# The outlook stage of a two-layer metaformer kernel: norm, outer and band moved in the step's order, loads moved to ScalarE's queue, the last stage's factors loaded and folded in two pieces

## The chip, the cores and the metric

One core of one Trainium2 chip runs the whole kernel. The metric is device time in microseconds for one execution, as a median of runs. The engines are named as the profile names them: PE (TensorE; PEld its weight loads), DVE (VectorE), ACT (ScalarE), POOL (GpSimd) and SP (SyncE, which here only issues DMAs). ACT and POOL can issue DMAs too; those stand in the engine's own stream of instructions, between its other work. The profile calls the DMA queue of SP q1, that of ACT q10 and that of POOL q0.

## The reference

The input is four images of 32 x 32 tokens with 384 channels, f32. Layer 0 adds a gated attention and a mixture of four experts; the change does not touch them. Layer 1 adds an outlook attention and a feed-forward network whose weights are Kronecker products. Cut to these two:

```python
x = x + _L1_conv_ref(_ln_c(x), L1_conv_Wv, L1_conv_Wa, L1_conv_Wo)
t = t + _L1_ffn_ref(_ln_t(t), c_fc_1, c_fc_2, c_proj_1, c_proj_2)

def _L1_conv_ref(x, Wv, Wa, Wo):          # 12 heads of 32, K = 3
    v = x @ Wv.T                          # padded by 1 on each side
    v_unf = patches(v)                    # the 3 x 3 neighbours of each pixel
    a = (x @ Wa.T).reshape(b, n, 12, 9, 9)
    attn = softmax(a * 32 ** -0.5)        # over the last 9
    out = einsum('bnhpq,bnqhd->bnphd', attn, v_unf)
    y = fold(out)                         # each of the 9 results is added at its pixel
    return y @ Wo.T

def _L1_ffn_ref(x, fc_1, fc_2, proj_1, proj_2):
    h = gelu(x @ kron(fc_1, fc_2).T)      # fc_1 1536 x 32, fc_2 1 x 12
    return h @ kron(proj_1, proj_2).T     # proj_1 32 x 1536, proj_2 12 x 1
```

## The kernel before

The 4096 tokens are 32 tiles of 128 (P), eight to an image (NB = 8, NT = 32). Four stages follow one another: `attention`, `experts`, `outlook` and `Kron.run`. Within outlook the order of instructions on every engine is the order in which the program emits them (`manual_schedule`, L2346); each engine works through its own list in order, and so do the queues of DMAs.

**What a tile goes through.** `norm` (L1866) writes xn, the layer norm of the tile, on DVE (L147). `turn` transposes it on PE (L155) and copies it to xnT on ACT (L156). `scores` multiplies xnT by wa in two halves of 486 columns (L1881) into the PSUM tiles ps_a0 and ps_a1, one buffer each, and subtracts the maximum of nine on DVE (L1887, L1888). `exps` is one exponential on ACT over the whole tile (L1895). `values` makes v (L1928, copied by ACT in L1932). `share` divides by the sums on DVE (L1901 to L1908) and sends thirds of the result, shifted by one image row (32 partitions), to tiles `up` and `down` with up to four DMAs on SP's queue (L1918, L1919, L1920, L1922): L1918 fills the last 32 rows of the tile before. `outer` copies two pieces of down and up into u on ACT (L1942, L1943), `inner` adds the three others on DVE (L1949 to L1951). `band` shifts u by one column on PE (L1960), masks it on DVE into co (L1968), writes co to a `room` in DRAM (L1975, 150 KB), waits for that on SP, and reads the room back as a band of 260 columns for each token (L1981, 1560 KB). `sort` copies the band, heads in pairs, into `own` with three ACT copies (L1991). `gather` multiplies v by own (L2004) and gathers into ps_y for a half image; with the last tile of a half it copies ps_y into y on ACT (L2013). `mix` multiplies y by wo (L2019), and `mixed` adds it to x (L2026).

**The loop** (L2039 to L2093) runs steps 0 to 36. Step i works on scores, exps, turn(i+1), values and share of tile i, on outer, inner and band of tile i-2, and on sort and gather of tile i-4 (LAG = 4). Mixes come in steps 9 to 15, 17 to 23, 25 to 31 and 33 to 36. Steps 8, 16, 24 and 32 have a gather for t = 4, the last tile of a first half, and two more at the step's end for the second half (L2075). From step 4 on, `add` adds the experts' results to the tiles 17 to 31 on DVE (L1844); POOL fetches them ahead (`ask`, L1541).

**Loads.** `loads` (L2339) is called at the start of a step: at step 1 x for image 1 and wo, at step 2 x for image 2 (from two sources), at step 5 x for image 3, at step 8 `kron.load` (L2117), which loads the factors of the last stage and folds two of them on DVE: f2sum (L2127), row (L2130) and wide (L2132). All of these DMAs stand on SP's queue, between those of share and band. The x tiles of image 0, wa and wv come on POOL's queue ahead of the loop.

**Semaphores of the DMAs.** DMAs on the queues of SP and ACT raise one of eight semaphores. A DMA which takes a semaphore again first waits on the engine that issues it, until the earlier DMA on that semaphore has landed.

The order before, cut to what the change moves:

```python
if 0 <= i - LAG < NT: sort(i - LAG)
if 0 <= i - 2 < NT: outer(i - 2)
if i < NT: scores(i, 0); scores(i, 1); exps(i)
if 0 <= i - 2 < NT: inner(i - 2)
if i + 1 < NT: xn = norm(i + 1)
...                                   # mixes, gather, turn(i + 1, xn), values, share
if 0 <= i - 2 < NT: band(i - 2)
```

Of the kernel before, what the change touches and what calls it, by code (L numbers as in the profile page):

```python
# [17 lines left out]
P = 128  # L18
# [3 lines left out]
NT = B * NB  # L22
# [1744 lines left out]
def outlook(net, wv, wa, wo, left, router, kron, loads):  # L1767
# [10 lines left out]
    tc, nc = net.tc, net.nc  # L1778
# [4 lines left out]
    with ExitStack() as ctx:  # L1783
# [82 lines left out]
        def norm(i):  # L1866
            xn = work.tile([P, C], FP, name="xn", tag="xn")
            net.ln_apply(xn, i, i, net.mv, net.rs)
            return xn
# [69 lines left out]
        def outer(i):  # L1939
            u = us[i] = work.tile([P, 6, 5, H3], FP, name="u", tag="u")  # L1940
            down, up = halves(i)
            nc.scalar.copy(u[:, :, 0, :], down[:, :, 0, :])  # L1942
            nc.scalar.copy(u[:, :, 4, :], up[:, :, 2, :])  # L1943
# [95 lines left out]
        for step in range(last + 1):  # L2039
            i = step  # L2040
            if step in loads:
                loads[step]()
            if 0 <= i - LAG < NT:
                sort(i - LAG)
            if 0 <= i - 2 < NT:
                outer(i - 2)
            if i < NT:
                scores(i, 0)
                scores(i, 1)
                exps(i)  # L2050
            if 0 <= i - 2 < NT:
                inner(i - 2)
            if i + 1 < NT:
                xn = norm(i + 1)
            done = []
            for one in mixes.pop(step, []):
                done.append(mix(*one))
                if len(done) == 2:
                    mixed(*done[0])
                    mixed(*done[1])  # L2060
                    gauged += [j for j, _ in done]
                    done = []
            if 0 <= i - LAG < NT:
                gather(i - LAG, 0 if (i - LAG) % NB < 5 else 1)
            if i + 1 < NT:
                turn(i + 1, xn)
            for one in done:
                mixed(*one)
                gauged.append(one[0])
            if i < NT:  # L2070
                values(i)
                share(i)
            if 0 <= i - 2 < NT:
                band(i - 2)
            if 0 <= i - LAG < NT and (i - LAG) % NB == 4:  # L2075
                gather(i - LAG - 1, 1)
                gather(i - LAG, 1)
            if coming:
                add()
                if left and left[0] % NB == 0 or not left and not coming:  # L2080
                    until = left[0] if left else NT
                    net.scale(first, until)
                    first = until
            if step >= 3 and left:
                ask(left.pop(0))
            while gauged and gauged[0] < kron.GT:
                kron.gauge(0, gauged.pop(0))
            if step == 2 * NB + LAG + 3:
                kron.begin(0)
            elif step > 2 * NB + LAG + 3 and t_kron < kron.GT:  # L2090
                for _ in range(2):
                    kron.shrink(0, t_kron)
                    t_kron += 1  # L2093
# [3 lines left out]
class Kron:  # L2097
# [8 lines left out]
    A, K = 32, 12  # L2106
# [10 lines left out]
    def load(self, fc1T, fc2, proj1T, proj2):  # L2117
        nc, A, K = self.nc, self.A, self.K
        const = self.const
        p2 = self.p2  # L2120
        for q in range(4):
            nc.sync.dma_start(out=self.wf[A * q : A * q + A, :], in_=fc1T)
        nc.sync.dma_start(out=self.wp, in_=proj1T.rearrange("(f p) a -> p f a", p=P))
        nc.sync.dma_start(out=self.f2, in_=fc2.rearrange("a b -> (a b)").partition_broadcast(P))
        nc.sync.dma_start(out=p2, in_=proj2.rearrange("a b -> (a b)").partition_broadcast(P))
        self.f2sum = const.tile([P, 1], FP, name="f2sum")
        nc.vector.tensor_reduce(self.f2sum, self.f2, AX.X, ALU.add)  # L2127

        row = const.tile([P, A], FP, name="row")
        nc.vector.tensor_reduce(row, self.net.ident.rearrange("p (q a) -> p a q", a=A), AX.X, ALU.add)  # L2130
        self.wide = const.tile([P, A, K], FP, name="wide")
        nc.vector.tensor_tensor(  # L2132
            self.wide, row.unsqueeze(2).to_broadcast([P, A, K]), p2.unsqueeze(1).to_broadcast([P, A, K]),
            ALU.mult,
        )
        self.xr = [const.tile([P, self.GT, A], FP, name=f"xr_{g}", tag=f"xr_{g}") for g in range(NT // self.GT)]
# [155 lines left out]
@with_exitstack  # L2292
def metaformer_kernel(
    ctx: ExitStack,
    tc: tile.TileContext,
    x, qkv_wT, gpT, proj_wT, proj_w, gate_w, gate_b, wup, wdown,
    WvT, WaT, WoT, fc1T, fc2, proj1T, proj2, out,
):
    cpool = ctx.enter_context(tc.tile_pool(name="cpool", bufs=1))
    small = ctx.enter_context(tc.tile_pool(name="small", bufs=2))  # L2300
    dram = ctx.enter_context(tc.tile_pool(name="dram", bufs=1, space=bass.MemoryType.DRAM))
    net = Net(tc, cpool, small)
    net.slots(dram)
    x1, x2 = (dram.tile([NT * P, C], FP, name=n) for n in ("x1", "x2"))
    unsafe = cpool.tile([1, 1], mybir.dt.int32, name="unsafe")

    def routing(outer):

        pool = outer.enter_context(tc.tile_pool(name="rt", bufs=1))
        ps_t = outer.enter_context(tc.tile_pool(name="ps_t", bufs=2, space=PSUM))  # L2310
        return Router(net, pool, cpool, lambda: ps_t.tile([P, 512], FP, name="ps_t", tag="pt"))

    def rest(router, done):

        with ExitStack() as late:

            pool = late.enter_context(tc.tile_pool(name="late", bufs=1, reuse_waits="tile"))
            kron = Kron(net, late, pool)
            net.xs = {}
            net.home(pool, 0)  # L2320
            wa, wv, wo = (
                pool.tile([P, KC, w.shape[-1]], FP, name=n, tag=n)
                for n, w in (("wa", WaT), ("wv", WvT), ("wo", WoT))
            )
            for b in range(1, B):
                net.home(pool, b)

            def fetch(b):
                first, last = b * NB, (b + 1) * NB
                net.load(x2, range(first, min(last, done)))  # L2330
                net.load(x1, range(max(first, done), last))

            def weigh(queue, tile_, w):
                queue.dma_start(out=tile_, in_=w.rearrange("(k p) o -> p k o", p=P))

            net.load(x2, range(NB), tc.nc.gpsimd)
            weigh(tc.nc.gpsimd, wa, WaT)
            weigh(tc.nc.gpsimd, wv, WvT)
            loads = {  # L2339
                1: lambda: (fetch(1), weigh(tc.nc.sync, wo, WoT)),  # L2340
                2: lambda: fetch(2),
                5: lambda: fetch(3),
                8: lambda: kron.load(fc1T, fc2, proj1T, proj2),
            }
            eng = mybir.EngineType
            with tc.manual_schedule(engines={eng.PE, eng.DVE, eng.Activation, eng.SP, eng.Pool}):  # L2346
                outlook(net, wv, wa, wo, range(done, NT), router, kron, loads)
            kron.run(out)

    with ExitStack() as outer:  # L2350
        router = routing(outer)
        eng = mybir.EngineType
        with tc.manual_schedule(engines={eng.PE, eng.DVE, eng.Activation, eng.SP}):
            left = attention(
                net, outer, router, x, x1, unsafe, qkv_wT, gpT, proj_wT, proj_w, gate_w, gate_b
            )
            done = experts(net, router, x1, x2, wup, wdown, left)
    rest(router, done)
    with tc.If(tc.nc.values_load(unsafe[0:1, 0:1], min_val=0, max_val=1) != 0):
        with ExitStack() as outer:  # L2360
            net.reside(outer.enter_context(tc.tile_pool(name="xpool", bufs=1)))
            net.load(x)
            general_attention(net, qkv_wT, gpT, proj_wT)
            net.store(x1)
            with ExitStack() as inner:
                router = routing(inner)
                for b, given in enumerate(gates(net, router.psum, gate_w, gate_b)):
                    for _ in router.route(b, *given):
                        pass
                    if b == B - 2:  # L2370
                        router.first()
                done = experts(net, router, x1, x2, wup, wdown, router.schedule)
        rest(router, done)
# [59 lines left out]
```

## Time and profile before

| | us |
|---|---|
| median of three runs (2775.6 to 2779.86) | 2779.47 |
| the profiled execution's own time | 2777.38 |
| its span, first to last instruction | 2774.9 |
| attention, to about | 1204 |
| experts, to about | 2250 |
| outlook, first turn to the start of step 9 | 2250.31 to 2371.64 |
| outlook, steps 9 to 31, to the last scores | 2371.64 to 2640.0 |
| outlook, steps 32 to 36 | 2640.0 to 2684.24 |
| Kron.run | 2684.24 to 2774.9 |

The mean granted clock of PE is 0.959. In these four last stretches PE is busy for 88.59 of 121.33, 264.17 of 268.36, 36.05 of 44.24 and 78.41 of 90.66 us, and the DMA engines for 60%, 57%, 48% and 20%.

How to read it. A timeline row gives the start, the time of the instruction or of a merged run of them, engine, line, operation and tiles; in brackets stands the time for which the engine had been idle, and what ended that. A row of the windows gives, for a stretch, its length, then busy time and number of instructions of PE, PEld, DVE, ACT and POOL, the granted clock, the share of the DMA engines' time and GB/s. "SPq" and "ACTq" rows are the issuing of DMAs: their time is that of the issue, not of the transfer. Ends of matmuls are modelled, so that the time from one run's start to the next one's is the safer figure.

### The profile page before, as it was taken

To read this page: it belongs to the slowest core of one execution; us is meant where nothing else is said; L and a number is where in the kernel's file an instruction comes from. 1 tells how busy PE (TensorE), PEld (TensorE's weight loads), DVE (VectorE), ACT (ScalarE), POOL (GpSimd) and SP (SyncE) were. 2 spreads that over 40 slices of the span, in tenths; PEclk is the share of its full clock that TensorE was granted. 3 is DMA by queue.
4 is the path that set the end of the run, shared out by engine and by line. 5 is a ranking of instruction groups with operands and counts; after the bars stand their busy time and mean duration, and the time that the engine had idled before them with its cause. 6 is when DMAs were issued, how large, how long until landed. Compare 5 with 4: busy or idle time off the path is not lost. (4 is left out here: it accounts for less than half of the span.)

```text
span 2774.9 us, 40133 instructions
## 1 busy us (share of the span) xinstructions
PE 2565.5 (92%) x14667; PEld 1558.3 (56%) x14667; DVE 1728.3 (62%) x4362; ACT 1301.9 (47%) x2119; POOL 417.8 (15%) x501
## 2 busy tenths in 40 slices
PE   6889999999999998789999999999999987999988
PEld 3323333333333332247889999999999953555532
DVE  1367778677778787647444544465455556887962
ACT  3778777677778777412221221121121123455455
POOL 1000000030003001413211112222222101110000
PEclk9989999999999998889999999999999999999989
DMA  5133434322322232454665545655655447565532
GB/s 108 33 103 92 108 86 126 95 60 63 96 73 64 59 107 69 133 175 160 230 238 207 202 170 216 232 194 217 237 205 211 175 145 221 165 201 175 173 110 93
DMA packets 215806, 404.13 MB, mean 146 GB/s; under 512 B 83344, under 2 KB 176848, under 8 KB 202544
## 3 DMA queue, kind: packets, MB, share of 16 engines
q1 hardware_dynamic: 184496, 187.82, 22.6%
q0 software_dynamic: 26960, 209.05, 22.0%
q10 hardware_dynamic: 4144, 4.61, 0.5%
q8 instruction: 118, 1.93, 0.3%
q14 instruction: 88, 0.72, 0.1%
HBM read 304.34 MB, written 49.00 MB: 127 GB/s over the span
## 5 line engine op out<-in xcount | busy, mean ns | idle before, releaser
L1702 ACT ACTIVATE h<-ps_h,up 128x256 f32<-128x256 f32 (+1 forms) x420 | 195.1, 465 | 825.3 <-PE ps_h L1697 823.7
L1697 PE MATMUL ps_h<-xbT,up 128*128 128x256 f32 (+1 forms) x2520 | 531.1, 371 | 2.5 <-ACT h L1702 1.8
L689 DVE CUSTOM_DVE_ANT_0 e<-e,rz,inv 128x1024 f32<-128x1024 f32 x384 | 475.3, 1274 | 47.3 <-DMA rz<-r_row 47.3
L1697 PEld LDWEIGHTS ps_h<-xbT,up 128*128 128x128 f32 x2520 | 462.6, 191 | 64.6 <-ACT h L1702 2.6
L637 ACT ACTIVATE e<-ps_s,ten 128x1024 f32<-128x1024 f32 x384 | 408.0, 1109 | 66.6 <-PE ps_s L627 40.1
L627 PE MATMUL ps_s<-q,k 32*128 32x512 f32 x1536 | 297.4, 671 | 51.5 <-ACT e L637 35.0
L645 PE MATMUL ps_o<-e,wv 128*32 128x512 f32 x1536 | 227.2, 666 | 40.3 <-DVE wv L696 38.8
L716 POOL DMA_DIRECT2D q<-po x96 | 76.2, 886 | 947.6 <-DMA q<-po 452.9
L645 PE MATMUL ps_z<-e,rt_ones 128*32 128x512 f32 x1536 | 217.1, 639 | 0.0
L373 ACT ACTIVATE below<-tk_left,tk_bound 128x1024 bf16<-128x1024 f32 (+1 forms) x160 | 184.4, 1152 | 52.4 <-DVE tk_bound L379 41.4
L1741 PE MATMUL ps_y<-wsum,hsum 128*128 128x192 f32 x1116 | 196.0, 329 | 9.5 <-DVE hsum L1657 5.2
L627 PEld LDWEIGHTS ps_s<-q,k 32*128 32x128 f32 x1536 | 92.8, 191 | 189.1 <-ACT e L637 92.0
L1741 PEld LDWEIGHTS ps_y<-wsum,hsum 128*128 128x128 f32 x1116 | 182.5, 191 | 13.2 <-DVE hsum L1657 6.6
L1881 PE MATMUL ps_a<-wa,xnT 128*128 128x486 f32 x384 | 162.1, 571 | 0.6 <-ACT xnT L156 0.6
L1745 DVE TENSOR_TENSOR y<-ps_y,y 128x192 f32<-128x192 f32 x155 | 55.5, 358 | 165.5 <-PE ps_y L1741 162.4
L645 PEld LDWEIGHTS ps_o<-e,wv 128*32 128x32 f32 x1536 | 31.5, 112 | 201.0 <-issue 66.1
L288 PE MATMUL ps_t<-xnT,wqkv 128*128 128x512 f32 x288 | 134.6, 607 | 2.4 <-ACT xnT L470 1.7
L1541 POOL DMA_INDIRECT yt<-yg,index x64 | 78.1, 1220 | 375.5 <-DVE x L1844 181.4
L645 PEld LDWEIGHTS ps_z<-e,rt_ones 128*32 128x32 f32 x1536 | 52.2, 117 | 132.0 <-issue 128.8
L1741 PE MATMUL ps_y<-down,h 128*128 128x192 f32 x744 | 126.0, 326 | 0.0
L1741 PEld LDWEIGHTS ps_y<-down,h 128*128 128x128 f32 x744 | 122.6, 190 | 1.6
L1991 ACT COPY own<-band 128x1040 f32<-128x1040 f32 x96 | 101.7, 1125 | 33.2 <-DMA band<-room 30.8
(398 smaller groups left out, 3576.7 us busy)
## 6 DMA issues: line engine op xcount, KB each, us to landing
band<-room SPq DMA_DIRECT2D x32, 1560.0 KB
rz<-r_row SPq DMA_DIRECT2D x48, 512.0 KB
yg<-y SPq DMA_DIRECT2D x67, 192.0 KB
q<-q SPq DMA_DIRECT2D x192, 64.0 KB
k<-k SPq DMA_DIRECT2D x192, 64.0 KB
room<-none SPq DMA_DIRECT2D x64, 192.0 KB
x<-x SPq DMA_DIRECT2D x35, 192.0 KB
o<-in_x_dram SPq DMA_DIRECT2D x33, 192.0 KB
```

Source lines behind the costliest of these rows:

```text
L288: nc.tensor.matmul(ps, lhsT=lhsT(k), rhs=rhs(k), start=k == 0, stop=k == KC - 1)
L373: nc.scalar.activation(junk[:n], left[:n], AF.Sign, bias=bound[:n], accum_out=over[:n])
L627: nc.tensor.matmul(ps[:, half * 512 : half * 512 + 512], lhsT=self.k4[r, u * P : (u + 1) * P], rhs=self.q4[r, :], start=True, stop=True,)
L637: nc.scalar.activation(e, ps, AF.Exp, bias=shift, scale=QK_SCALE)
L645: nc.tensor.matmul(ps[r : r + 32, :], lhsT=lhsT(odd), rhs=self.es[2 * u + odd][:, half * 512 : half * 512 + 512], start=u == 0, stop=u == ...
L689: nc.vector.tensor_tensor_reduce(self.es[m], self.es[m], self.rz, 1.0, self.im["inv"][:, m, self.h : self.h + 1], ALU.mult, ALU.add, self. ...
L1541: self.nc.gpsimd.indirect_dma_start(out=y, out_offset=None, in_=self.net.yg[: first_row(self.complete(i // NB)), :], in_offset=bass.Indire ...
L1697: nc.tensor.matmul(ps, lhsT=up[:, o : o + P], rhs=xbT[:, k, :size], start=k == 0, stop=k == KC - 1,)
L1702: nc.scalar.activation(hs[f // 3][:, f % 3, :size], ps, AF.Gelu, bias=up[:, KC * HID + f : KC * HID + f + 1])
L1741: nc.tensor.matmul(ps, lhsT=left[f], rhs=right[:, f, :], start=f == 0, stop=f == HF - 1)
L1881: nc.tensor.matmul(pa[:, :HW_], lhsT=xnTs[i][:, k, :], rhs=wa[:, k, hh * HW_ : (hh + 1) * HW_], start=k == 0, stop=k == KC - 1,)
L1991: nc.scalar.copy(own[:, pairs], m.rearrange("p t (n h) -> p n t h", h=2)[:, pairs])
```

## The change

Six edits, all in outlook and in what it loads. In the loop `outer(i - 2)` comes ahead of `sort(i - 4)`; `norm(i + 1)` comes ahead of the scores; in the steps past the last tile (32 and 33) `band` comes ahead of `gather`. The loads at steps 1, 2, 5 and 8 are issued by ACT on its own queue. `kron.load` is cut in two: the DMAs stay at step 8, the three DVE operations become `fold` and move to step 14.

```diff
--- before.py
+++ after.py
@@ -2040,18 +2040,18 @@
             i = step
             if step in loads:
                 loads[step]()
+            if 0 <= i - 2 < NT:
+                outer(i - 2)
             if 0 <= i - LAG < NT:
                 sort(i - LAG)
-            if 0 <= i - 2 < NT:
-                outer(i - 2)
+            if i + 1 < NT:
+                xn = norm(i + 1)
             if i < NT:
                 scores(i, 0)
                 scores(i, 1)
                 exps(i)
             if 0 <= i - 2 < NT:
                 inner(i - 2)
-            if i + 1 < NT:
-                xn = norm(i + 1)
             done = []
             for one in mixes.pop(step, []):
                 done.append(mix(*one))
@@ -2060,6 +2060,8 @@
                     mixed(*done[1])
                     gauged += [j for j, _ in done]
                     done = []
+            if i >= NT and i - 2 < NT:
+                band(i - 2)
             if 0 <= i - LAG < NT:
                 gather(i - LAG, 0 if (i - LAG) % NB < 5 else 1)
             if i + 1 < NT:
@@ -2070,7 +2072,7 @@
             if i < NT:
                 values(i)
                 share(i)
-            if 0 <= i - 2 < NT:
+            if 0 <= i - 2 and i < NT:
                 band(i - 2)
             if 0 <= i - LAG < NT and (i - LAG) % NB == 4:
                 gather(i - LAG - 1, 1)
@@ -2119,10 +2121,14 @@
         const = self.const
         p2 = self.p2
         for q in range(4):
-            nc.sync.dma_start(out=self.wf[A * q : A * q + A, :], in_=fc1T)
-        nc.sync.dma_start(out=self.wp, in_=proj1T.rearrange("(f p) a -> p f a", p=P))
-        nc.sync.dma_start(out=self.f2, in_=fc2.rearrange("a b -> (a b)").partition_broadcast(P))
-        nc.sync.dma_start(out=p2, in_=proj2.rearrange("a b -> (a b)").partition_broadcast(P))
+            nc.scalar.dma_start(out=self.wf[A * q : A * q + A, :], in_=fc1T)
+        nc.scalar.dma_start(out=self.wp, in_=proj1T.rearrange("(f p) a -> p f a", p=P))
+        nc.scalar.dma_start(out=self.f2, in_=fc2.rearrange("a b -> (a b)").partition_broadcast(P))
+        nc.scalar.dma_start(out=p2, in_=proj2.rearrange("a b -> (a b)").partition_broadcast(P))
+
+    def fold(self):
+        nc, A, K = self.nc, self.A, self.K
+        const, p2 = self.const, self.p2
         self.f2sum = const.tile([P, 1], FP, name="f2sum")
         nc.vector.tensor_reduce(self.f2sum, self.f2, AX.X, ALU.add)
 
@@ -2327,8 +2333,8 @@
 
             def fetch(b):
                 first, last = b * NB, (b + 1) * NB
-                net.load(x2, range(first, min(last, done)))
-                net.load(x1, range(max(first, done), last))
+                net.load(x2, range(first, min(last, done)), tc.nc.scalar)
+                net.load(x1, range(max(first, done), last), tc.nc.scalar)
 
             def weigh(queue, tile_, w):
                 queue.dma_start(out=tile_, in_=w.rearrange("(k p) o -> p k o", p=P))
@@ -2337,10 +2343,11 @@
             weigh(tc.nc.gpsimd, wa, WaT)
             weigh(tc.nc.gpsimd, wv, WvT)
             loads = {
-                1: lambda: (fetch(1), weigh(tc.nc.sync, wo, WoT)),
+                1: lambda: (fetch(1), weigh(tc.nc.scalar, wo, WoT)),
                 2: lambda: fetch(2),
                 5: lambda: fetch(3),
                 8: lambda: kron.load(fc1T, fc2, proj1T, proj2),
+                14: kron.fold,
             }
             eng = mybir.EngineType
             with tc.manual_schedule(engines={eng.PE, eng.DVE, eng.Activation, eng.SP, eng.Pool}):
```

In the changed kernel's lists, ACT issues the seven loads of step 8 (four of wf, wp, f2, p2) after the copy of v(7) and ahead of outer(6), sort(4) and exps(8). SP's list is the old one without the loads. PE's list differs only in steps 32 and 33. On the eight semaphores, the fourth wf load takes that of the first one, wp and f2 take those of the L1918 and L1919 copies of step 7, and p2 that of the second wf load.

## The prediction

> **What bounds the kernel now.** I read three views, in this order: the slices of the page, a table of windows with one row for each step of the outlook stage (from the start of its scores matmuls to the next), and the timelines of the engines where a row is longer than its work. From the page, two rows of 40 slices of 69.4 us:
>
> ```profile
> PE   6889999999999998789999999999999987999988
> PEclk9989999999999998889999999999999999999989
> ```
>
> PE is busy nearly everywhere; of the stretches that the change touches, slice 33 (2289 to 2359 us) is the weakest, with 7 tenths. The windows: columns are the stretch, its length, busy time of PE, PEld, DVE, ACT, POOL, granted clock, DMA share, GB/s.
>
> ```profile
> 2251.45:2260.84 9.39, 7.45 (x22) 3.72 (x23) 4.66 (x10) 2.74 (x3) 2.43 (x3) 1.00 0.33 93
> 2260.84:2270.12 9.28, 7.35 (x23) 3.62 (x22) 6.66 (x14) 1.97 (x3) 0.00 (x0) 1.00 0.61 197
> 2270.12:2282.46 12.34, 9.75 (x29) 5.43 (x27) 9.49 (x20) 3.10 (x7) 0.00 (x0) 0.86 0.66 209
> 2282.46:2295.00 12.54, 9.95 (x29) 5.48 (x28) 7.91 (x18) 2.81 (x5) 0.00 (x0) 0.86 0.51 169
> 2295.00:2305.85 10.85, 9.43 (x53) 5.19 (x52) 7.38 (x17) 5.08 (x9) 0.00 (x0) 1.00 0.55 186
> 2305.85:2316.71 10.86, 9.79 (x54) 5.20 (x53) 9.60 (x23) 5.18 (x8) 2.52 (x3) 1.00 0.68 215
> 2316.71:2328.42 11.71, 9.78 (x54) 5.20 (x52) 9.33 (x23) 5.51 (x8) 2.15 (x2) 1.00 0.82 251
> 2328.42:2343.71 15.29, 11.54 (x54) 5.99 (x52) 10.55 (x25) 5.64 (x9) 2.51 (x3) 0.89 0.72 245
> 2343.71:2371.64 27.93, 13.04 (x102) 7.46 (x100) 12.00 (x29) 7.47 (x12) 2.25 (x3) 0.69 0.51 134
> ...
> 2383.57:2454.35 70.78, 70.78 (x349) 39.10 (x348) 64.77 (x154) 36.76 (x54) 13.61 (x14) 1.00 0.66 211
> 2454.35:2466.82 12.47, 10.37 (x101) 5.82 (x99) 11.67 (x29) 7.27 (x12) 2.16 (x2) 1.00 0.65 207
> 2466.82:2549.55 82.73, 82.73 (x410) 45.70 (x407) 66.91 (x158) 42.15 (x63) 3.10 (x4) 1.00 0.55 180
> 2549.55:2563.72 14.17, 12.07 (x101) 6.86 (x99) 10.57 (x27) 10.26 (x15) 0.00 (x0) 0.88 0.51 166
> ```
>
> The first nine rows are steps 0 to 8. Steps 10 to 31, the last four rows and what follows to 2640, are PE without a gap (70.78 of 70.78), except steps 16 and 24. So the change can earn only in steps 0 to 8, 16, 24 and at the end. The longest hole, step 8, in the timelines of DVE, PE and SP's queue:
>
> ```profile
> 2359.39 0.17 DVE L2127 TENSOR_REDUCE f2sum<-f 128x1 f32<-128x12 f32 x1 [12.96 <-DMA f<-in_fc_dram]
> ```
> ```profile
> 2364.15 0.87 PE L155 MATMUL ps_tr<-ident,xn 128*128 128x128 f32 x3 [14.89 <-DVE xn L147]
> ```
> ```profile
> 2350.01 3.59 SPq L2124 DMA_DIRECT2D f<-in_fc_dram  x1
> ```
>
> DVE stands 12.96 us at f2sum until a load of 6 KB lands, which was issued behind the band DMA (1560 KB) and the wf and wp loads; max, subtraction and norm of the step queue behind it, and PE stands 14.89 us.
>
> **Warm PE work of a step**, from rows of the chain: scores 4.90, turn 0.35, values 1.94, band 0.91, gather 1.2 to 1.5 (t=4: 0.5 and 1.5), mix 1.94. Floors: steps 0 and 1 7.2 each, 2 and 3 8.1, 4 to 7 9.3, 9.65, 9.65, 9.3, steps 8, 16, 24 10.1.
>
> **Norm ahead of the scores, steps 0 to 3.** xn is then there when PE has finished the scores, so the waits 1.93, 1.93, 2.59, 2.59 of L155 go. What is late next is xnT: behind the scores' end come max and subtraction (1.36), exps 1.01 and the copy 0.48 on ACT, 2.95 in all with hand-overs. PE has turn and values, 2.3, in steps 0 and 1, with band 3.2 in steps 2 and 3. So step 0 takes 8.15 (9.39 before), step 1 8.15 (9.28), steps 2 and 3 8.2 (12.34, 12.54; there also turn and values at the slow clock go, 0.87+3.07 against 0.35+1.94). Gain 1.24+1.13+4.14+4.34 = 10.9. Bounds: 2.4, if steps 2 and 3 get nothing because their up copies land late, to 13 (43.55 less the floors 30.6). DVE's 0.47 for norm now precedes the max; in steps 10 to 31 the max waits for PE (37.3 us in 40 waits), which hides it; uncovered it would cost 0.47 a step.
>
> **Clock.** PE ran slow after idles of 2.59 (values: six in 3.28) and not after 1.93 (2.10); I charge 1.5 us for each new hole above 2.5. The Trainium skill, "TensorE: Matmul & The Clock Gate", Part 1, says that the clock falls after an idle window of about 3.4 us, free-running; by that the hole I expect in step 4 would cost 0 and the sum be 1.5 better, but the rows with 2.59 speak against it.
>
> **Loads on ACT's queue, outer ahead of sort, steps 4 to 7.** The earlier steps now run into the band DMA. A band takes 6.2 to 6.9 from issue to landing (2666.38 to 2672.58; 2311.61 to 2318.5) and SP's queue lands in order: the up copy issued at 2328.54 landed at 2335.23, 0.15 after the band issued at 2326.42. With steps of 8.2, share(2) ends at 2278.8, room(0) is issued at 2280.6, band(0) at 2283.0, it lands at 2289.4, and the first up copy of step 3, issued at 2286.2, lands behind it at 2289.6. In step 4 ACT does outer (0.47), then sort (3.17), then exps; before, sort came first. So own(0) is ready only at 2293.3, with the scores done at 2288.9: PE waits 4 to 5, and step 4 takes 13.8 plus 1.5 of slow clock. From there each step hangs on the ring exps 1.0, share 2.9 to its first third, up copy 2 to 3.5, outer 0.5, sort 3.2: 9.6 to 11.1. I take 10.75, 11.3, 9.7 for steps 5, 6, 7 (fetch(3) beside step 5). Sum 47.0 against 48.7: gain 1.7. Bounds: every step as step 4, 55.2, a loss of 6.5; the floors, 37.9, a gain of 10.8. The loads' own issue costs ACT 0.4 to 0.6 each, beside its waits for DVE.
>
> **Step 8.** DVE's wait goes. ACT now issues seven DMAs ahead of outer(6), sort(4) and exps(8). The trace shows them on SP: 1.86+0.43+3.59+0.45 = 6.3. Beyond that, in the built kernel the fourth wf load waits on the semaphore of the first, wp and f on those of the up copies of step 7. On my clock: v(7) done at 2329.1, wf landed 2333, wp 2334.6, f 2338.6, p 2339; outer and sort to 2342.7 (gather's first third at 2340.6, scores done at 2334.4); exps and three y copies (1.54) and xnT to 2345.2; values, band and the late gathers with 1.5 to 3 of slow clock to 2349: 19.5 against 27.93, gain 8.4. Bounds: ACT standing as long as DVE did, gain 0; no hole, 17.8. I choose between them by the issue rows.
>
> **Steps 16 and 24.** Waits of 2.10 on xn go (in 24 also values at 3.33). ACT's chain then ends at xnT, 2463.2+0.5, beside PE's work; PE's 10.1 plus 0.7 makes 10.8: gain 1.6 and 3.4, together 5 (0 to 6.4).
>
> **Steady steps, outer ahead of sort.** The up copy lands 1.94 after issue at least (2271.53 to 2273.47); its reader, ACT L1943, started unhindered 3.29 after (2634.75 to 2638.04), 4.29 and 5.06 in others, which bounds it above. Taking the step whose scores start at 2431.36: issue at -0.70, outer 0.47, sort 3.17; the gather starts at +6.91 behind mix and wants its last third 1.0 later, so landings up to 4.97 cost nothing. Price 0, bound 2 us over the stage. **fold** at step 14 adds 0.17+0.35+0.56 = 1.1 on DVE, which is free 6.0 of 70.78 in those steps: 0, uncovered 1.1.
>
> **Last two bands.** Band(30) waits for inner(30), whose place on DVE behind the shrink rows (to 2650.6) is unchanged. Band(31)'s room write is issued up to 1 us earlier, but queues behind band(30) (2658.73 to 2665.38), and the last band is issued at 2666.38 today: gain 0.4 (-2.7, by which sort(28) is later, to 0.9).
>
> **Sum.** 10.9+1.7+8.4+5+0.4 = 26.4. The profiled execution took 2777.38 (span 2774.9 and 2.5 around it), 2.1 less than the median 2779.47: 2777.4-26.4+2.1 = 2753. Differences under 0.2% (5.6 us) count as the same.
>
> **Rivals.** (1) Forecast, 2746 to 2760: 0.54. (2) ACT's stall replaces DVE's: step 8 gains 0 to 3; 2758 to 2762: 0.16. For: the semaphores above; against: only the loads' issue, not f's landing, holds ACT. (3) The bands do not collide: steps 4 to 7 near their floors and step 8 at 14: 11+9+14+5 = 39, 2741: 0.13. For: the loads leave SP's queue; against: 6.4 of band, 2.4 of room and the share copies fill about 10 us of each step. (4) The other queue frees nothing: fetch(2) and fetch(3) delay the up copies as on one queue (7.71 with fetch(3), against 1.94), about 3 us in each of four steps: 12 lost, 2765: 0.09. So says the Trainium skill, "DMA: Bandwidth & Descriptors", section "Issuing engines are not separate DMA queues": only issue time is saved. Its section "Queues, rings and completion order" has the engines alternate between queues by packet, by which a small copy passes a large load; no row here shows either. (5) Slower: outer waits for every up copy in all 22 steps 10 to 31 as long as the two late ones (7.71, 6.69; mean 7.2): sort ends at -0.70+7.2+3.7 = +10.2 against +7.9, 2.3 late, 50 lost: 2803. It decides from 27/22 = 1.2 a step, a landing of 6.2. Against: the bounds 3.29 to 5.06. 0.04. (6) No difference, 2779, gains of (1) eaten by the worst of steps 4 to 8: 0.04.
>
> Faster 0.92, same 0.04, slower 0.04. The range 2740 to 2767 leaves out (5), (6) and about a tenth at the lower edge of (3) and beyond.
>
> **What would show it.** Right: no wait of f2sum, no L155 wait on xn in steps 0 to 3, 16, 24; a PE hole in step 4 ended by own L1991; in step 8 a PE hole of 5 to 8 us ended by own, with ACT's DMA issues ahead; steps 10 to 31 gapless at 11.7. Wrong: PE holes in steps 10 to 31 behind own, an ACT hole over 10 us in step 8, or steps 4 to 7 under 10 us.

## The result, and the profile after

| | before | after |
|---|---|---|
| median of 6 runs each, us | 2779.08 (2775.6 to 2785.98) | 2753.47 (2744.2 to 2759.54) |
| the profiled execution | 2777.38 | 2747.41 |
| its span | 2774.9 | 2745.4 |

The ratio of the medians is 0.9905, with a 95% interval of 0.9891 to 0.9919. The forecast was 2753.0, and the profiled execution is 29.97 us shorter: 1.03 before the outlook stage, 25.63 in it (from the first scores to the first matmul of the last stage: 432.79 to 407.16), 2.85 in the last stage, and 0.47 around the span. Only the 25.63 lie where the change acts; the last stage has the same instructions and ran at a granted clock of 0.94 against 0.89 before.

The slices of the page after, PE and granted clock:

```profile
PE   6889999999999998679999999999999998999988
PEclk9989999999989998779999999999999999999999
```

Slice 33 (2265 to 2334 us now) has 8 tenths where 7 stood, its neighbours 9 each; what is left of the holes is in the table by step. Windows after, steps 0 to 8, then 9, 16 and 24; columns as before.

```profile
2250.42:2258.45 8.03, 7.42 (x22) 3.61 (x22) 3.05 (x5) 2.69 (x4) 2.44 (x3) 1.00 0.37 109
2258.45:2266.47 8.02, 7.42 (x21) 3.61 (x22) 6.62 (x14) 1.76 (x4) 0.00 (x0) 1.00 0.91 289
2266.47:2274.97 8.50, 8.45 (x28) 4.53 (x28) 7.37 (x17) 2.23 (x6) 0.00 (x0) 1.00 0.77 241
2274.97:2283.58 8.61, 8.41 (x28) 4.63 (x28) 7.91 (x20) 2.54 (x7) 0.00 (x0) 1.00 0.22 56
2283.58:2299.34 15.76, 11.27 (x53) 5.77 (x52) 10.70 (x25) 5.46 (x10) 0.00 (x0) 0.89 0.68 235
2299.34:2309.08 9.74, 9.74 (x53) 5.21 (x52) 8.07 (x19) 5.63 (x9) 2.52 (x3) 1.00 0.84 252
2309.08:2324.01 14.93, 11.47 (x54) 5.41 (x52) 10.93 (x26) 5.41 (x8) 2.15 (x2) 0.89 0.84 275
2324.01:2333.42 9.41, 9.41 (x53) 5.22 (x52) 7.90 (x20) 5.22 (x7) 2.51 (x3) 1.00 0.61 166
2333.42:2351.91 18.49, 12.53 (x101) 6.91 (x99) 12.81 (x30) 7.93 (x14) 2.25 (x3) 0.82 0.86 250
2351.91:2363.69 11.78, 11.78 (x62) 6.45 (x58) 8.79 (x20) 4.53 (x7) 2.05 (x2) 1.00 0.55 184
...
2434.61:2444.96 10.35, 10.35 (x102) 5.89 (x100) 9.37 (x23) 6.95 (x12) 2.16 (x2) 1.00 0.71 238
2527.65:2538.00 10.35, 10.35 (x101) 5.87 (x99) 7.88 (x21) 9.93 (x17) 0.00 (x0) 1.00 0.60 199
```

PE's first busy figure is the step's length in steps 5, 7, 9, 16 and 24: no hole there. Holes are left in steps 4, 6 and 8. f2sum now runs in step 14 (2414.92, 0.13 us) and waits for nothing. The timelines of ACT and PE in step 8 show what stands in the place of its 12.96 us:

```profile
2332.71 5.53 ACTq L2124 DMA_DIRECT2D wf<-in_fc1T_dram  x4
2339.90 0.39 ACTq L2125 DMA_DIRECT2D wp<-in_proj1T_dram  x1
2340.33 0.87 ACTq L2126 DMA_DIRECT2D f<-in_fc_dram  x1
...
2341.80 0.28 ACT L1942 COPY u<-down 128x108 f32<-128x108 f32 x1 [8.61 <-issue]
```
```profile
2343.32 0.45 PE L2004 MATMUL ps_y<-own,v 128*32 128x66 f32 x8 [4.84 <-ACT own L1991]
```

ACT issues the seven loads from 2332.71 on and does nothing else until 2341.80; outer, sort and the gather follow, and PE has stood 4.84. In step 6, which the forecast had without a hole, SP's queue shows a room write and the band that waits for it:

```profile
2300.91 0.54 SPq L1975 DMA_DIRECT2D room<-co  x1
2308.36 0.33 SPq L1981 DMA_DIRECT2D band<-room  x1
```

Band(2) could be issued only 7.45 us after the write of its room. The 1.5 MB load of image 3, issued by ACT at 2298.78, ran beside it. The up copy issued at 2309.97, behind that band, took 6.03 to land; outer and sort waited for it, and the gather of step 6 then stood 3.23 for own:

```profile
2317.36 0.81 PE L2004 MATMUL ps_y<-own,v 128*32 128x260 f32 x8 [3.23 <-ACT own L1991]
```

### The profile page after: what moved, and what is told of

It reads as the page before. It is cut to its first block, busy times and chain, and to the rows that moved or that the text cites. A ratio compares the mean times of both kernels' runs of the same rounds, so it can differ in the third digit from the quotient of the medians.

```text
span 2745.4 us, 40115 instructions
## 1 busy us (share of the span) xinstructions
PE 2558.5 (93%) x14667; PEld 1555.1 (57%) x14667; DVE 1726.9 (63%) x4362; ACT 1302.3 (47%) x2119; POOL 416.8 (15%) x501
## 3 DMA queue, kind: packets, MB, share of 16 engines
q8 instruction: 118, 1.93, 0.3%
## 5 line engine op out<-in xcount | busy, mean ns | idle before, releaser
L1881 PEld LDWEIGHTS ps_a<-wa,xnT 128*128 128x128 f32 x384 | 71.1, 189 | 74.2 <-issue 70.2
```

The lines of the kernel that those rows point to most:

```text
L1881: nc.tensor.matmul(pa[:, :HW_], lhsT=xnTs[i][:, k, :], rhs=wa[:, k, hh * HW_ : (hh + 1) * HW_], start=k == 0, stop=k == KC - 1,)
```

## The experiments

All of them were run in three groups, each beside runs of the kernel before on the same chip. What comes ahead of the outlook stage varies between chips and executions (its first scores start at 2250 to 2306 us), so I read each run by the lengths in its profiled execution. The stretch is that from the first scores to the first matmul of the last stage; the tail is its part from the scores of tile 31 on. Steps 9 to 15, 17 to 23 and 25 to 30 are gapless and equally long in all runs unless said.

| run | median, before beside it | ratio, 95% | steps 0-3 | 4-7 | 8 | 16+24 | tail | stretch |
|---|---|---|---|---|---|---|---|---|
| before | | | 43.55 | 48.71 | 27.93 | 26.64 | 49.12 | 432.79 |
| after | 2753.5, 2779.1 | 0.9905 (0.9891-0.9919) | 33.16 | 49.84 | 18.49 | 20.70 | 48.20 | 407.16 |
| e1 fold alone | 2766.0, 2785.0 | 0.9930 (0.9908-0.9952) | 42.06 | 44.41 | 14.18 | 26.58 | 49.70 | 413.72 |
| e2 norm alone | 2769.8, 2785.0 | 0.9936 (0.9914-0.9958) | 32.76 | 52.37 | 25.06 | 20.72 | 50.02 | 417.67 |
| e3 loads on SP | 2756.0, 2785.0 | 0.9893 (0.9873-0.9914) | 32.75 | 50.53 | 11.64 | 20.72 | 49.05 | 404.51 |
| e4 sort first | 2765.4, 2785.0 | 0.9919 (0.9896-0.9942) | 33.41 | 50.95 | 21.63 | 20.71 | 50.42 | 413.88 |
| e5 factors on POOL | 2800.7, 2826.5 | 0.9922 (0.9903-0.9941) | 34.68 | 50.93 | 18.93 | 20.70 | 48.29 | 410.31 |
| e6 image 3 later | 2794.5, 2826.5 | 0.9892 (0.9873-0.9912) | 33.75 | 48.30 | 17.94 | 20.71 | 48.50 | 405.99 |
| e7 bands back | 2801.7, 2826.5 | 0.9920 (0.9900-0.9941) | 33.29 | 50.76 | 18.19 | 20.70 | 49.20 | 408.91 |
| e8 POOL, SP, later | 2797.9, 2826.5 | 0.9908 (0.9887-0.9929) | 32.76 | 45.92 | 20.72 | 20.71 | 48.31 | 405.23 |
| e9 loads spread | 2755.2, 2786.4 | 0.9881 (0.9860-0.9902) | 32.77 | 49.49 | 11.10 | 21.69 | 49.91 | 401.86 |
| e10 spread, sort first | 2746.9, 2786.4 | 0.9856 (0.9835-0.9876) | 32.75 | 49.40 | 10.34 | 20.70 | 48.80 | 398.77 |
| e11 spread on ACT | 2753.7, 2786.4 | 0.9879 (0.9859-0.9898) | 32.76 | 48.90 | 11.55 | 22.34 | 51.12 | 403.47 |
| e12 spread, late gather | 2753.0, 2786.4 | 0.9879 (0.9858-0.9901) | 32.74 | 45.97 | 11.27 | 21.55 | 50.42 | 398.72 |

The step lengths of a row come from one execution. How much of them varies without a cause in the kernel can be read where two kernels have the same instructions. Up to step 7 e1 is the kernel before, and yet its steps 0 to 3 take 1.49 and its steps 4 to 7 4.30 less. Up to step 31 e7 is the changed kernel; its step 4 takes 16.64 against 15.76, each other step agrees within 0.3. Step 4, the same in all runs with norm first (but for the order of outer and sort, and for e12), takes 15.41 to 18.43, by a hole of 3.5 to 5.6 and by how long PE is at the slow clock after it. The tail takes 48.2 to 51.1 in runs whose tail is the same instructions. Differences below 3 us in step 4 and in the tail tell nothing.

### The fold alone (e1), norm alone (e2)

```diff
@@ e1: before, with kron.load cut in two
+                14: kron.fold,
@@ e2: before, with norm moved
+            if i + 1 < NT:
+                xn = norm(i + 1)
             if i < NT:
                 scores(i, 0)
```

> The kernel before with one edit: the three DVE operations of kron.load move from step 8 to step 14; the loads stay on SP's queue at step 8. My account: the hole of step 8 was DVE's wait at f2sum alone, so step 8 falls from 27.9 to 12.5 to 13.5 us and nothing else moves: about 2764 (15 less than before). That is more than the changed kernel won in step 8 (27.93 to 18.49, 9.4), the rest being what ACT pays there for issuing the loads. Rival: SP's issue of the seven loads (6.3 us) holds back the share and band copies of the next steps, so that steps 8 to 10 keep holes of 5 us or more: about 2769 or above.

> The kernel before with one edit: norm(i+1) ahead of the scores. My account: steps 0 to 3 fall from 43.6 to about 33, steps 16 and 24 from 26.6 to about 20.7, steps 4 to 7 gain or lose up to 6 because the band copies now collide, the hole of step 8 stays at 12 to 13 on DVE: 2762 to 2770. Rival: it is the loads on another queue that freed steps 2 and 3; then with the loads still on SP's queue steps 2 and 3 stay above 11 us each, and the time is 2771 or more.

The fold alone brings 19.07 of stretch, 13.75 of it in step 8, with every load still on SP's queue; the rest lies in steps 0 to 7, which the edit does not touch. Step 8 stays at 14.18, above the expected 12.5 to 13.5, with a wait of 2.10 on xn and the slow clock behind it. Steps 9 and 10 have no hole (11.78, 11.66), so the rival falls. Norm alone brings 15.12: 10.79 in steps 0 to 3, 5.92 in steps 16 and 24, but step 4 becomes 16.05 and step 7 16.82, and f2sum's wait stays (step 8 25.06). Steps 2 and 3 are 8.35 and 8.30 there, with the loads on SP's queue: so norm alone, not the other queue, closed them.

### The loads back on SP's queue (e3), and sort ahead of outer (e4)

```diff
@@ e3: after, in fetch, weigh of wo and kron.load
-            nc.scalar.dma_start(out=self.wf[A * q : A * q + A, :], in_=fc1T)
+            nc.sync.dma_start(out=self.wf[A * q : A * q + A, :], in_=fc1T)
@@ e4: after
-            if 0 <= i - 2 < NT:
-                outer(i - 2)
             if 0 <= i - LAG < NT:
                 sort(i - LAG)
+            if 0 <= i - 2 < NT:
+                outer(i - 2)
```

> The changed kernel with all loads back on SP's queue. My account: in step 8 ACT no longer stands for 9 us at the issue, so step 8 falls from 18.5 to 13 or less; in steps 2, 3, 5, 6 the up copies queue behind the x loads and cost 0 to 6 in all: 2744 to 2753, not slower than the changed kernel. Rival: the other queue is what earned in steps 0 to 7, and without it the kernel is 5 to 10 slower than the changed one, 2758 to 2763.

> The changed kernel with sort again ahead of outer on ACT. My account: the holes of PE in steps 4 and 6 end at a sort that stood behind outer, which stood behind an up copy landing about 0.2 to 0.5 us after the band itself; sort first ends them 0.5 to 1 earlier each, and steps 10 to 31 stay gapless either way: 1 to 3 less than the changed kernel, about 2751. Rival: outer ahead of sort earns something, because band and inner get u earlier; then sort first is 3 or more slower, 2756.

With the loads on SP's queue the stretch is 2.65 shorter than after the change. Windows of this run, steps 8 and 10:

```profile
2345.00:2356.64 11.64, 10.75 (x102) 5.90 (x100) 10.84 (x25) 6.95 (x12) 2.16 (x2) 1.00 0.76 245
...
2368.41:2383.15 14.74, 12.15 (x59) 6.14 (x58) 10.28 (x25) 5.44 (x8) 2.16 (x2) 1.00 0.82 261
```

Step 8 loses its hole (18.49 to 11.64), and 3.07 come back in step 10 (11.67 after), where ACT waits for an up copy that took 7.59 from issue (2368.25) to landing, behind a band that SP could issue only at 2367.81, after the loads. The account had no loss there. So the move to ACT's queue cost about 7 in step 8 and saved 3 in step 10; in steps 0 to 3 it cost 0.4.

With sort first, step 8 is 3.14 longer (ACT's timeline):

```profile
2356.42 3.13 ACT L1991 COPY own<-band 128x1040 f32<-128x1040 f32 x3 [11.07 <-DMA wf<-in_fc1T_dram]
```

The account expected 1 to 3 less and is refuted. The rival's sign came, its reason did not show: sort starts in both kernels once ACT has issued the last load (in the changed kernel 0.4 later, behind outer), and what is later here is the up copy of step 7 for which ACT stands at the issue of wp. It took 7.64 to land, 5.25 in the changed kernel. Whether the order brought that, one execution does not tell; the three with outer first and these loads on ACT's queue (after, e6, e7) have 17.94 to 18.49 in step 8. The other 3.6 of the stretch lie in step 4 and the tail (0.95 and 2.2), which vary as much without it, and 0.4 in steps 2, 3 and 6. The intervals of e4 and the changed kernel overlap, so that outer ahead of sort makes the kernel faster is not shown.

### What ends step 8: the factors on POOL's queue (e5)

```diff
@@ after, the seven loads of kron.load
-            nc.scalar.dma_start(out=self.wf[A * q : A * q + A, :], in_=fc1T)
+            nc.gpsimd.dma_start(out=self.wf[A * q : A * q + A, :], in_=fc1T)
```

> As the changed kernel, but the seven loads of step 8 are issued by POOL on its queue. Measured from the first scores to the first Kron matmul (407.16 in the changed kernel, with step 8 18.49). Theory: what step 8 has above 10 to 11 us is ACT standing at the seven issues and at their semaphores; then step 8 is 11 to 12.5, steps 9 to 15 stay at 11.6 to 11.8, and the stretch is 399 to 402. Rival: it is the transfers, on whichever queue, that make the band and the up copies land late; then step 8 or steps 9 and 10 together stay 3 us or more above that, with a PE hole ended by own, and the stretch is 403 to 407.

Here ACT issues nothing in step 8, and the step still takes 18.93. Its timeline, POOL's, SP's queue, ACT and PE:

```profile
2380.44 2.08 POOL L2124 DMA_DIRECT2D wf<-in_fc1T_dram  x4
...
2387.08 0.54 SPq L1918 DMA_DIRECT2D up<-attn  x1
...
2394.63 0.28 ACT L1943 COPY u<-up 128x108 f32<-128x108 f32 x1 [8.84 <-DMA up<-attn]
...
2395.97 0.45 PE L2004 MATMUL ps_y<-own,v 128*32 128x66 f32 x8 [5.07 <-ACT own L1991]
```

ACT stands 8.84 again, now openly for the up copy, issued at 2387.08 and landed 7.53 later, behind band(4) (issued 2380.96) on its own queue and beside the loads on the other. The theory that ACT's standing at the issues sets step 8 falls; the rival's mechanism holds. The stretch of 410.31 is outside both ranges, by steps 2 and 4 (1.51 and 1.03 longer than after the change).

In the changed kernel outer reads the same copy at 2341.99 without a wait, which hides that ACT had waited for it before. The chain of work that ended last, after (start, time, what), shows it: the issue of wp takes the semaphore of that copy and waits until it has landed.

```profile
2334.63 5.25 DMA up<-attn
...
2339.90 0.39 ACTq L2125
```

The copy landed at 2339.88, 6.5 us into the step; without any issue ACT could not have begun outer's second copy before that. What the issues themselves cost beyond it is at most the 2.1 us to 2341.99. A sum says the same: in the changed kernel's step 8 the transfers of ACT's queue took 25.8% of 19 us of all DMA engines, 4.9 us, where step 8 without the loads needs 7.8 (0.75 of 10.34 in e10) to 9.0 (0.81 of 11.10 in e9). Together that is 12.7 to 13.9, more than PE's 10.1.

Why SP's queue is better at the same step: there the loads come behind band(5), issued at 2351.32 in e3, 6.3 us into the step and after the up copies of tile 7 (2346.23, 2346.82); on ACT's and POOL's queues they start 0.7 and 5.4 us ahead of the step and overtake those copies, which land 5.25 and 7.53 after their issue, against 1.87 in e3. The queue acts here as a place in the order; the same queue with the loads at another place of step 8 was not run. The Trainium skill, "DMA: Bandwidth & Descriptors", "Issuing engines are not separate DMA queues", has it that another engine's queue saves only time at the issue, and the trace agrees as far as it goes: neither queue made step 8 shorter (18.93 and 18.49 against 11.64).

### What makes step 6 long: image 3 later (e6); the last bands (e7)

```diff
@@ e6: after
-                5: lambda: fetch(3),
+                9: lambda: fetch(3),
@@ e7: after, without the band ahead of the gather
-            if i >= NT and i - 2 < NT:
-                band(i - 2)
-            if 0 <= i - 2 and i < NT:
+            if 0 <= i - 2 < NT:
                 band(i - 2)
```

> As the changed kernel, but image 3 of x is loaded at step 9 and not at step 5. Theory: the hole of 3.23 us in step 6 (step 14.93 long) is made by the 1.5 MB load on ACT's queue, beside which room(2) took 7.45 us to land; without it step 6 is 9.5 to 11, step 5 is as before (9.7), and the steps 9 and 10, which now have the load beside them, lose at most 2 together, since PE's work there covers more; the stretch from the first scores to the first Kron matmul is 402 to 405 against 407.16. Rival: the hole comes from the late band of step 4, whose delay returns every second step; then step 6 stays at 14 or above, and the stretch is 406 to 409.

> As the changed kernel, but the last two bands stand behind the gather again. Theory: that edit is worth 0.4 to 1 us, by band(31)'s earlier room write; the stretch from the scores of tile 31 to the first Kron matmul is 48.6 to 49.2 against 48.20. Rival: the band transfers queue one behind the other, and the end does not move; 48.0 to 48.4. Steps 0 to 31 as in the changed kernel, within 1 us.

Windows of e6, steps 6 and 7:

```profile
2366.26:2376.43 10.17, 9.95 (x53) 5.10 (x52) 9.40 (x23) 5.47 (x8) 2.16 (x2) 1.00 0.57 168
2376.43:2388.20 11.77, 9.88 (x54) 5.01 (x53) 10.19 (x24) 5.22 (x7) 2.51 (x3) 1.00 0.74 243
```

Step 6 is 4.76 shorter, and band(2) is issued 3.00 us after its room write instead of 7.45; step 7 gives back 2.36, and steps 9 and 10, now with the whole load beside them, lose nothing (11.78, 11.67). That the load makes step 6 long is shown; moving it is worth half of what step 6 gains, and the stretch, 405.99, ends above the expected 402 to 405. Which small transfer the load holds up depends on the queue, the length of the step does not: in e3, with the load on SP's queue, room(2) took 3.18, the up copy issued behind the load 5.49, and step 6 14.75. The Trainium skill, "DMA: Bandwidth & Descriptors", section "Queues, rings and completion order", weighed in the prediction, has the DMA engines alternate between queues, by which the 150 KB write would pass the load; 7.45 against 3.00 says that it does not pass unhindered.

In e7 the tail is 49.20 against 48.20, in the theory's range, but five runs with the bands early have 49.05 to 51.12. PE stood 5.19 and 0.98 us there with the bands early, 3.02 and 3.19 with them late: the wait has moved. A gain of the edit is not shown.

### All of it together (e8), and the loads cut up (e9 to e12)

```diff
@@ e8: e5 with x and wo on SP's queue, and
-                5: lambda: fetch(3),
+                9: lambda: fetch(3),
@@ e9: after, every load on SP's queue; kron.load issues one part a call
-                5: lambda: fetch(3),
-                8: lambda: kron.load(fc1T, fc2, proj1T, proj2),
-                14: kron.fold,
+                20: kron.fold,
             }
+            for n in range(4):
+                loads[9 + n] = lambda n=n: net.load(x1, range(3 * NB + 2 * n, 3 * NB + 2 * n + 2), tc.nc.sync)
+            for n in range(6):
+                loads[13 + n] = lambda n=n: kron.load(fc1T, fc2, proj1T, proj2, n)
@@ e10: e9 with e4's order. e11: e9 with tc.nc.scalar and nc.scalar. e12: e9, and in step 4 alone
                 values(i)
+                if i == LAG:
+                    gather(0, 0)
                 share(i)
```

> Norm ahead of the scores, outer ahead of sort, the two bands and the fold at step 14 as in the changed kernel; the loads of x and wo on SP's queue as before the change, that of image 3 at step 9 and not at step 5, the seven loads of step 8 on POOL's queue. If the terms add up (step 6 4 to 5 us, step 8 6 to 7 us below the changed kernel), the stretch from the first scores to the first Kron matmul is 395 to 399 against 407.16 and 404.51 with all loads on SP. Rival: image 3 on SP's queue at step 9 pushes the band and up copies behind it and opens a hole in step 10 or 11 as the loads of step 8 did (14.74); then 399 to 403.

> As the changed kernel, but with every load on SP's queue as before the change, and the large ones cut up: image 3 of x in four pairs of tiles at steps 9 to 12, the four wf loads at steps 13 to 16, wp at 17, f2 and p2 at 18, the fold at 20. Measured from the first scores to the first Kron matmul (407.16 in the changed kernel, 404.51 with all loads on SP at their old steps). Theory: steps 6 and 8 are long because a load of 1.5 MB or 1 MB is in flight together with a band and holds up the up copies and the room write, whatever its queue; loads of 0.2 to 0.4 MB in steps that have cover cost nothing. Then step 6 is 9.5 to 11, step 7 9.4 to 11.8, step 8 10.3 to 11.8, steps 9 to 31 as in the changed kernel, and the stretch is 395 to 399. Rival: on one queue each load stands in front of an up copy; steps 9 to 18 lose 0.3 to 1 us each, and the stretch is 400 to 405.

> As the run with the loads spread, but with sort ahead of outer, as before the change. Theory: the order of outer and sort matters only where a load collides with the band, as in step 8 with the loads on ACT's queue (21.63 against 18.49); here step 8 is within 0.5 us of the spread run, and the stretch is 0 to 2 us longer, most of that in the tail. Rival: outer ahead of sort is worth its 6.7 us everywhere; the stretch is 4 to 7 us longer than in the spread run.

> As the run with the loads spread, but the spread loads are issued by ACT on its queue (those of steps 1 and 2 stay on SP's). Theory: what costs time is the size of a load beside a band, not its queue; the stretch is within 1 us of the spread run, step 8 within 0.5. Rival: on a queue of its own each load runs beside the band ahead of the up copies and delays them, or ACT stands at the issue; steps 9 to 18 lose 0.2 us or more each, the stretch is 2 to 6 us longer.

> As the run with the loads spread, but in step 4 alone, the first with a gather, PE does turn and values ahead of the gather. Theory: PE's hole of 3.5 us in step 4 waits for band(0) and the sort behind it, so 2.3 us of turn and values fill it and the slow clock after it (1 to 1.5 us) goes with the hole; step 4 is 12 to 13.5 against 15.5 to 16.7, the steps after it are unchanged, and the stretch is 2.5 to 4 us shorter than in the spread run. Rival: what step 4 gains comes back in step 5 or 6, since band(2) and the up copies are set by DVE and the DMAs; the stretch is within 1 us of the spread run.

e8 missed both expectations: steps 4 to 7 fell to 45.92, but step 8 rose to 20.72, with ACT 9.72 at an up copy that took 8.57 to land. Taken with e5 this says it twice: POOL's queue does not help. The whole load of image 3, on SP's queue at step 9, cost nothing here either (steps 9 and 10 11.78 and 11.68).

e9 does what its theory says in steps 6 and 8 (windows of the run):

```profile
2324.76:2334.89 10.13, 9.94 (x54) 5.10 (x53) 9.36 (x23) 5.44 (x8) 2.16 (x2) 1.00 0.55 153
...
2346.08:2357.18 11.10, 10.53 (x101) 5.85 (x99) 10.32 (x25) 6.96 (x12) 2.15 (x2) 1.00 0.81 263
```

It loses 0.97 in step 16, beside a wf load, and 0.1 in steps 9 to 15. Its stretch of 401.86 is outside the expected 395 to 399, by step 4 (18.43) and the tail (49.91), whose instructions are those of the changed kernel. Leaving step 4 and the tail out, the changed kernel has 343.20, e3 338.82, e9 333.52.

By the same measure e10 has 334.56, e11 335.06, e12 335.56. So with the loads cut up, the order of outer and sort leaves 1.0 (with sort first step 7 is 3.0 longer, steps 8 and 16 0.8 and 1.0 shorter), which one execution each does not resolve. Neither expectation of e10 came: its stretch is 3.09 shorter, and step 8 differs by more than 0.5. e11 is 1.5 above e9, but 0.54 and 0.45 of that lie in steps 7 and 8, ahead of the first load that differs; only the 0.65 in step 16 can be the queue's. The theory's main point, that the queue matters little, stands; its range of 1 us and the rival's steps (0.2 or more lost in each of 9 to 18) were both missed. e10 has the shortest median, 2746.86, 8.3 below e9; only 3.1 of this is in the stretch of the profiled runs, by step 4 and the tail (4.1), and the intervals overlap. e10 is faster than before and, as far as ratios from two chips can say it, than the changed kernel (its interval ends at 0.9876, the other begins at 0.9891); that it beats e9 is not shown.

e12's step 4 shows that PE's hole there can be filled (window and PE's timeline):

```profile
2294.18:2306.92 12.74, 10.56 (x54) 5.64 (x53) 8.22 (x20) 5.36 (x10) 0.00 (x0) 0.95 0.70 218
```
```profile
2302.73 0.55 PE L2004 MATMUL ps_y<-own,v 128*32 128x194 f32 x8 [1.23 <-ACT own L1991]
```

The hole is 1.23 where e9 had 5.59; 5.69 are gained in step 4 and 2.34 given back in steps 5 to 8. Theory and rival each hold for a part. But e9's step 4 (18.43) is the longest of all runs; measured from e10's, the shortest, the gain there is 2.67.

## Why the prediction was right, and where not

| term | forecast gain | measured | 
|---|---|---|
| steps 0 to 3 | 10.9 | 10.39 |
| steps 4 to 7 | 1.7 | -1.13 |
| step 8 | 8.4 | 9.44 |
| steps 16 and 24 | 5 | 5.94 |
| steady steps | 0 | 0.07 |
| tail | 0.4 | 0.92 |
| sum | 26.4 | 25.63 |

The measured gains compare one execution with one. In e1 the order of before took 5.8 less in steps 0 to 7; with those lengths steps 0 to 3 would show a gain of 8.9 and steps 4 to 7 a loss of 5.4.

- **Norm ahead of the scores: right.** Steps 0 and 1 are 0.12 and 0.13 shorter than said, 2 and 3 0.30 and 0.41 longer. ACT waits 5.03 and 4.10 for up copies in steps 2 and 3 and nobody stands behind it. The excess comes with the loads on ACT's queue: with them on SP's, steps 0 to 3 took 32.74 to 32.77 in seven runs, on ACT's 33.16 to 34.68. The 37.3 us in 40 waits of the max, given for steps 10 to 31, are those of the whole outlook stage; steps 10 to 31 have about 18 us in 25. That norm is hidden there holds all the same (0.07).
- **Step 4: right in place, cause and size.** 13.8 and 1.5 of slow clock were said; it took 15.76, with a hole of 3.55 ended by own, behind an up copy that ACT waited 7.08 for. With sort first the hole is the same (3.61), since sort waits for the band itself.
- **Steps 5 to 7: the failed term.** 10.75, 11.3 and 9.7 were said, 9.74, 14.93 and 9.41 came. I charged the load of image 3 to the up copies of step 5; it hit the room write of band(2), one link earlier in the ring, and showed a step later as a hole with slow clock. The profile before has such a row: behind the same load the room write of tile 3 was issued at 2319.02 and its band at 2326.42, 7.40 later, and ACT waited 6.93 for that band in step 7, the one of 15.29. Of the signs of being wrong, "steps 4 to 7 under 10 us" came for steps 5 and 7 alone.
- **Step 8: right in size, wrong in cause.** 19.5 and a hole of 5 to 8 ended by own were said; 18.49 and 4.84 came. That ACT's standing at its issues sets it fell with e5, and the chain after has the up copy, 5.25 to its landing, as what that standing ended on; I had named that semaphore, but not that outer needs the same copy. I had taken the loads for a cost of issue and semaphores and given their transfer, 4.9 us of all DMA engines beside a band, no price. The fold alone gains 13.75 in this step; the move to ACT's queue made it 6.85 longer than the same order with the loads on SP's (e3) and saved 3.07 in step 10.
- **Rival (4) was right in its mechanism and wrong in its place and price.** The other queue freed nothing, but steps 2 and 3, where I had priced it, lost only 0.5; it cost in steps 6 and 8. Rival (3), 2741, has about the number of e10, whose median is 39.6 below its before, but not its mechanism: steps 4 to 7 take 49.40 there, far from their floors of 37.9, and step 8 10.34 and not 14.
- **Outer ahead of sort: price 0 in the steady steps, right.** Elsewhere nothing is shown: e4 lost 3.14 in step 8 without it, in one execution, and with the loads cut up 1.0 is left.
- **fold at step 14: 0, right.** Last two bands: 0.4 was said; the sign is not resolved.
- **Clock: 1.5 for a hole above 2.5 was good for step 4** (PE busy 11.27 against 9.74 for step 5's like work), a little low for step 6 (11.47 against 9.4 to 9.95) and within the 1.5 to 3 said for step 8 (12.53 against 10.35). It is no fixed price: e7, with the same instructions, had 12.62 in step 4.

The sum came out within 0.8 because step 8, the tail and steps 16 and 24 were 2.5 better and steps 0 to 7 3.3 worse. That is in part luck: errors cancelled, and the steps of one execution vary by more than 0.8. The step lengths, not the sum, show what was understood.

## What to carry to other kernels

Moving a large load to another engine's queue changes when it starts, not whether it shares the DMA engines: sum the transfers of the step against PE's work there, and look at which small copies it now overtakes. A wait that is shown at an issue may hide a second one that ends at the same time; take the first away, or follow the chain through it, before you name it the cause. Put a load where PE's own work covers it: here 2.5 MB, moved from steps 5 and 8 to steps 9 to 18 and cut into nine pieces and two small ones, took 9.7 us less than in two lumps on ACT's queue, and 5.3 less than in two lumps on SP's (333.52 against 343.20 and 338.82). Moving and cutting were not parted: the 1.5 MB of image 3 cost nothing at step 9 in one lump (e6, e8), and the 1 MB of factors in one lump at a later step was not run.

## What the runs showed of the hardware that was not expected

The slow clock depends on more than the length of the idle before it. PE's timeline in e1, steps 1 and 2:

```profile
2276.85 0.52 PE L155 MATMUL ps_tr<-ident,xn 128*128 128x128 f32 x3 [1.93 <-DVE xn L147]
2277.21 3.79 PE L1928 MATMUL ps_v<-wv,xnT 128*128 128x384 f32 x6
...
2288.48 0.52 PE L155 MATMUL ps_tr<-ident,xn 128*128 128x128 f32 x3 [2.59 <-DVE xn L147]
2288.84 2.10 PE L1928 MATMUL ps_v<-wv,xnT 128*128 128x384 f32 x6
```

After an idle of 1.93 the six values matmuls take 3.79, after one of 2.59 2.10, the other way round from the rows of before on which the prediction built its 2.5. Step 16 and step 24, with the same wait of 2.10, took 12.47 and 14.17 before and 14.11 and 12.47 in e1. That equal idles end differently would fit the free-running window of which the Trainium skill tells ("TensorE: Matmul & The Clock Gate", Part 1), but no run here shows the window; that an idle must be as long as its 3.4 us does not fit an idle of 1.93. The prediction took from that length that the hole of step 4 would cost nothing, though it expected 4 to 5 us there, which is longer. A hole thus cost between 0 and 3 us beyond its length (PE busy 12.80 in step 4 of e4, 9.74 in the like work of step 5), and equal instructions differ by it (step 4 11.27 after, 12.62 in e7).
